# Selective scan of the last image: two-bank PSUM tiles of 1024 elements in place of four single banks

## The chip, the cores and the metric

The kernel runs on one core of one Trainium2 chip. The metric is the device time of one execution in microseconds (us); the time before is 25678.4 us, the median of three runs (25666.2 to 25685.54).

## The reference

The input is four images of 128 x 128 positions and 128 channels in float32. Two layers follow each other, each with a group norm in front and a residual around it.

```
x = x + L0(gn(x))     # deformable 3x3 convolution, two groups of 64 channels, bilinear sampling
x = x + L1(gn(x))     # two selective-scan (Mamba) blocks
```

The second layer takes each row of an image as one sequence: x has the shape (4, 128, 128, 128), and the reference reshapes it to 512 sequences of 128 steps. One scan block computes, for 256 inner channels and 16 states s,

```
delta = softplus(dt @ dtw + dtb);  dA = exp(delta * A[s])
h[t]  = dA[t] * h[t-1] + (delta*u)[t] * B[t, s]        # the scan
y[t]  = sum over s of h[t] * C[t, s];   out = ((y + u*D) * silu(res)) @ ow
```

## The kernel before

Layer 0 of image b + 1 is interleaved with layer 1 of image b. When the last image (b = 3) is in layer 1, no layer 0 is left, and layer 1 has the core to itself.

Layer 1 works in jobs. A job is one block of four rows (SR = 4, so TB = 512 positions) and one of the two scan layers. An image has 32 blocks, so the last image has 64 jobs. The jobs of two blocks alternate: block A layer 0, block B layer 0, A layer 1, B layer 1. Channels lie on the 128 partitions, in two halves c = 0, 1 (NC = 2).

- `pre` prepares a job: the input projection with the short convolution folded in (tile `pu`, L542, two groups of eight matmuls), silu (`u`), the gate `g` (`pr`, L557), the projections to dt, B and C (`pdb`, L566), their turned copy `bt`, then softplus in the steps L591 to L596 on ScalarE. Four dependent VectorE instructions end it: L600 (`e`), L601 and L602 (`de`, the delta), and L603 (`du`, delta times u).
- In the last image `turn_du` (L508) then turns `du` with TensorE (`pdu`) and ScalarE copies it to `duts` (L520).
- `main` does the scans of a job in eight quarters q of two states n (NQ = 2). A quarter has one of three `da` buffers. ScalarE fills it with exp (L639, four runs) and zeroes the first column of each row (L634), so that a scan starts afresh at each row.
- For n = 0 GpSimd multiplies `duts` by B into `xs` (L658, four instructions), for n = 1 ScalarE does (L656). TensorE turns `xs` into PSUM tile `px` (L663, four 128 x 128 transposes for each half c), and VectorE scans over 512 elements (L665).
- VectorE multiplies the quarter's 2048 results by C (L668), and TensorE adds them up in `y` (L133, sixteen transposes that accumulate).
- The tail of a job: gate (L689), turn back (`pyg`), output projection (`pout`), and for the second layer the residual and the store. The next job's `y` begins with `ddiag` times `u` (L618).

While `main` of a job runs, the `pre` of the next one is advanced by a step after each quarter, so that L600 to L603 stand near the sixth quarter and the pu groups near the first two. The tile framework decides the order on each engine's queue when the kernel is built, so the queues do not follow the program text strictly; each then runs in order and waits on semaphores. The next job's first `xs` need its `duts`, and so its L603.

PSUM has eight banks of 512 float32 per partition. In the kernel before, `ps` (two banks, tag "t") and `psa` (two banks, tag "acc") belong to layer 0; in the last image `px` takes them over, one bank per tile: `psa` for n = 0, `ps` for n = 1. `ps1` (two banks) serves `pre` and the tail, and `psy` (two banks) holds `y`. In the first three images a scan reads SBUF tile `hs` instead of PSUM and takes a quarter's 2048 elements at once (L679).

The layout of `da` is [c, n, s, t] in the kernel before, for every image.

Of the kernel before, what the change touches and what calls it, by code (L numbers as in the profile page):

```python
# [10 lines left out]
F32 = mybir.dt.float32  # L11
I32 = mybir.dt.int32
AF = mybir.ActivationFunctionType
ALU = mybir.AluOpType
PSUM = bass.MemoryType.PSUM
DRAM = bass.MemoryType.DRAM

P = 128
# [4 lines left out]
SR = 4  # L23
TB = SR * P
NGT = 4
NPA = 2
NL = 2
NC = 2
NS = 16
NQ = 2  # L30
# [34 lines left out]
def block_kernel(ctx: ExitStack, tc: tile.TileContext, a: dict, out: bass.AP):  # L65
    nc = tc.nc
# [9 lines left out]
    ident = const.tile([P, P], F32, name="ident")  # L76
# [13 lines left out]
    cw = ctx.enter_context(tc.tile_pool(name="w", bufs=1))  # L90
    small = ctx.enter_context(tc.tile_pool(name="small", bufs=1))
    pb = ctx.enter_context(tc.tile_pool(name="l0b", bufs=1))
    ps = ctx.enter_context(tc.tile_pool(name="l0ps", bufs=2, space=PSUM))
    psa = ctx.enter_context(tc.tile_pool(name="l0psa", bufs=NPA, space=PSUM))
    p2 = ctx.enter_context(tc.tile_pool(name="l1p2", bufs=1))
    pd = ctx.enter_context(tc.tile_pool(name="l1d", bufs=3, space=DRAM))
    ps1 = ctx.enter_context(tc.tile_pool(name="l1ps", bufs=4 - NPA, space=PSUM))
# [11 lines left out]
    offb, cbias, one, zero = misc[:, 0:1], misc[:, 1:2], misc[:, 2:3], misc[:, 4:]  # L109
# [21 lines left out]
    def add_transposed(o, v, start, stop):  # L131

        nc.tensor.matmul(o, v, ident, is_transpose=True, start=start, stop=stop, skip_group_check=True)  # L133
# [341 lines left out]
    NDA = 3  # L475
    n_da = [0]
    das, lm = [], []
# [13 lines left out]
    def next_h():  # L491
        n_h[0] += 1
        return hps[n_h[0] % NH]

    def load_x1(blk, nm):
        b, off = divmod(blk * TB, H * W)
        t = p2.tile([P, TB], F32, tag="x1t", name=f"x1t_{nm}", bufs=2)
        nc.sync.dma_start(t, x1[b][:, off : off + TB])
        return t

    def in_last(blk):

        return blk * SR // H == B - 1

    duts = []
    n_dut = [0]

    def turn_du(st, nm):  # L508

        if not duts:  # L510
            duts.append(lm[0].tile([P, 2, SR, NC * P], F32, tag="hs", name="duts"))
        n_dut[0] += 1
        dut = duts[0][:, n_dut[0] % 2]
        for k in range(SR // 2):
            pt = ps1.tile([P, 2, NC, P], F32, tag="t", name=f"pdu_{nm}_{k}")
            for i in range(2):
                for c in range(NC):
                    o = (2 * k + i) * P
                    nc.tensor.transpose(pt[:, i, c, :], st["du"][:, c, o : o + P], ident)
            nc.scalar.copy(dut[:, 2 * k : 2 * k + 2], pt.rearrange("p s c d -> p s (c d)"))  # L520
        st["dut"] = dut
# [88 lines left out]
    def main(st, l):  # L610

        blk = st["blk"]
        nm = f"{blk}_{l}"

        y = psy.tile([P, SR, NC, P], F32, tag="y", name=f"y_{nm}")
        for i in range(SR):
            for c in range(NC):
                nc.tensor.matmul(  # L618
                    y[:, i, c], st["u"][:, c, i * P : (i + 1) * P], ddiag[:, l, c, :],
                    start=(i % 2 == 0 and c == 0), stop=False, skip_group_check=True,  # L620
                )
        if in_last(blk) and "dut" not in st:
            turn_du(st, nm)
        for q in range(NS // NQ):
            bc = []
            for w in range(in_last(blk), 2):
                t = lm[0].tile([P, NQ, TB], F32, tag=f"bc{w}", name=f"bc{w}_{nm}_{q}", bufs=2)
                n0 = w * NS + q * NQ
                nc.sync.dma_start(t, st["bcd"][n0 : n0 + NQ, :].partition_broadcast(P))
                bc.append(t)  # L630
            da = das[n_da[0] % NDA]
            n_da[0] += 1

            nc.scalar.copy(da.rearrange("p c n s t -> p (c n s) t")[:, :, 0], zero)  # L634
            for c in range(NC):
                dv = st["delta"][:, c].rearrange("p (s t) -> p s t", s=SR)
                for n in range(NQ):
                    s = q * NQ + n
                    nc.scalar.activation(  # L639
                        da[:, c, n, :, 1:], dv[:, :, 1:], AF.Exp, scale=aneg[:, l, c, s : s + 1]  # L640
                    )
            dc = da.rearrange("p c n s t -> p c (n s t)")
            cv = bc[-1].rearrange("p n t -> p (n t)").unsqueeze(1).to_broadcast([P, NC, NQ * TB])
            if in_last(blk):


                for n in range(NQ):
                    s = q * NQ + n

                    xs = (lm[0] if n else pb).tile(  # L650
                        [P, SR, NC * P], F32, tag="bc0" if n else "gw", name=f"xs_{nm}_{s}", bufs=2
                    )
                    for i in range(SR):
                        bv = st["bt"][:, i, s : s + 1]
                        if n:
                            nc.scalar.activation(xs[:, i], st["dut"][:, i], AF.Copy, scale=bv)  # L656
                        else:
                            nc.gpsimd.tensor_scalar(xs[:, i], st["dut"][:, i], bv, None, ALU.mult)  # L658
                    for c in range(NC):
                        pool, tag = (ps, "t") if n else (psa, "acc")  # L660
                        px = pool.tile([P, SR, P], F32, tag=tag, name=f"px_{nm}_{s}_{c}")
                        for i in range(SR):
                            nc.tensor.transpose(px[:, i, :], xs[:, i, c * P : (c + 1) * P], ident)  # L663
                        dn = da[:, c, n].rearrange("p s t -> p (s t)")
                        nc.vector.tensor_tensor_scan(  # L665
                            dn, dn, px.rearrange("p s t -> p (s t)"), 0.0, ALU.mult, ALU.add
                        )
                nc.vector.tensor_tensor(dc, dc, cv, ALU.mult)  # L668
            else:
                hs = lm[0].tile([P, NC, NQ, TB], F32, tag="hs", name=f"hs_{nm}_{q}")  # L670

                for n in range(NQ):
                    nc.vector.scalar_tensor_tensor(  # L673
                        hs[:, :, n, :], st["du"], one,
                        bc[0][:, n].unsqueeze(1).to_broadcast([P, NC, TB]),
                        op0=ALU.mult, op1=ALU.mult,
                    )
                df = da.rearrange("p c n s t -> p (c n s t)")
                nc.vector.tensor_tensor_scan(  # L679
                    df, df, hs.rearrange("p c n t -> p (c n t)"), 0.0, ALU.mult, ALU.add  # L680
                )
                nc.vector.scalar_tensor_tensor(dc, dc, one, cv, op0=ALU.mult, op1=ALU.mult)  # L682
            for c in range(NC):
                for n in range(NQ):
                    for i in range(SR):
                        add_transposed(y[:, i, c], da[:, c, n, i, :], False, q == NS // NQ - 1 and n == NQ - 1)
            yield
        gt = st["g"]
        nc.vector.tensor_tensor(gt, y.rearrange("p s c d -> p s (c d)"), gt, ALU.mult)  # L689
        yg = p2.tile([P, NC, TB], F32, tag="yg", name=f"yg_{nm}")  # L690
        for c in range(NC):
            pt = ps1.tile([P, SR, P], F32, tag="t", name=f"pyg_{nm}_{c}")
            for i in range(SR):
                nc.tensor.transpose(pt[:, i, :], gt[:, i, c * P : (c + 1) * P], ident)  # L694
            nc.scalar.copy(yg[:, c], pt.rearrange("p s t -> p (s t)"))
        po = ps1.tile([P, TB], F32, tag="t", name=f"pout_{nm}")
        if l < NL - 1:
            for c in range(NC):
                nc.tensor.matmul(po, ow[:, l, c, :], yg[:, c], start=(c == 0), stop=(c == NC - 1))  # L699
            st["h"] = next_h()  # L700
            nc.scalar.copy(st["h"][:, :, DCONV - 1 :], po.rearrange("p (s t) -> p s t", s=SR))
        else:
            x1t = load_x1(blk, f"o{nm}")
            for i in range(SR):
                o = po[:, i * P : (i + 1) * P]
                nc.tensor.matmul(o, x1t[:, i * P : (i + 1) * P], ident, start=True, stop=False)
                for c in range(NC):
                    nc.tensor.matmul(  # L708
                        o, yg[:, c, i * P : (i + 1) * P], ow[:, l, c, :], start=False, stop=(c == NC - 1)
                    )  # L710
            ot = p2.tile([P, NC, TB], F32, tag="w1", name=f"ot_{nm}")[:, 0].rearrange("p (r c) -> p r c", r=SR)
            nc.scalar.copy(ot.rearrange("p r c -> p (r c)"), po)
            b, row = divmod(blk * SR, H)
            nc.sync.dma_start(out[b, row : row + SR].rearrange("r w c -> w r c"), ot)
# [121 lines left out]
```

## Time and profile before

| What | Value |
|---|---|
| Median of the runs | 25678.4 us (25666.2 to 25685.54) |
| Profiled execution | 25712.72 us, its span 25710.9 us |
| Mean granted TensorE clock | 0.891 of full speed |
| TensorE matmul busy | 20188.7 us, 79% of the span |
| VectorE busy | 20940.3 us, 81% |
| ScalarE busy | 16846.0 us, 66% |
| GpSimd busy | 18041.7 us, 70% |
| Scans of the last image (L665) | 2048 of 1202 ns on the mean, 21386 to 25693 us |

The engines are PE (TensorE matmul), PEld (its weight loads), DVE (VectorE), ACT (ScalarE), POOL (GpSimd) and SP (SyncE, which issues transfers). A line of the groups view gives the line of code, the engine, the operation, output and inputs, sizes and count; then the busy time in us and the mean duration of one in ns; and behind the second bar the idle time of the engine just before them, with what ended it. A line of the timeline gives the start, the length in us and, in brackets, the idle time before it and its releaser; neighbours of one kind are merged and counted with x. A duration is longer than the distance between two starts, since neighbours overlap a little.

### The profile page before, as it was taken

The numbers are of one execution on the slowest core, as the hardware profiler recorded it, in microseconds if no ns is written. First come the engines' busy times: TensorE is split into PE (matmuls) and PEld (weight loads), VectorE is DVE, ScalarE is ACT, GpSimd is POOL, SyncE is SP. The second block draws the span as 40 slices with busy tenths as digits, with TensorE's granted clock in tenths as the row PEclk, the third lists the DMA queues.
The fourth block names the chain that finished last, engine by engine and source line by source line (L and its number), as shares of the span: only waits on it lengthen the run. The fifth ranks groups of instructions, "written<-read, shape, count | busy, mean of one in ns | idle before, by whom it ended". The sixth has DMA issues, their size and how long they took to land. (4 is left out here: it accounts for less than half of the span.)

```text
span 25710.9 us, 302728 instructions
## 1 busy us (share of the span) xinstructions
PE 20188.7 (79%) x106276; PEld 12610.6 (49%) x106276; DVE 20940.3 (81%) x13054; ACT 16846.0 (66%) x40304; POOL 18041.7 (70%) x11270
## 2 busy tenths in 40 slices
PE   4676667888888887888888887888888877888787
PEld 2333334454554554554454454554554545666666
DVE  2212216999999999999999999999999998888888
ACT  2444445666676666666666666666676667888887
POOL 3666666788788885788788875888788864555555
PEclk7888888999998988999999988999999988999999
DMA  4434433444444544444444444444444442222222
GB/s 123 135 101 133 124 104 128 155 159 157 158 157 156 162 157 144 156 158 158 159 158 158 158 156 144 158 157 156 160 158 157 159 146 76 71 69 70 70 69 68
DMA packets 1530710, 3470.01 MB, mean 135 GB/s; under 512 B 243283, under 2 KB 717651, under 8 KB 1529052
## 3 DMA queue, kind: packets, MB, share of 16 engines
q1 hardware_dynamic: 1086812, 2242.08, 27.3%
q0 software_dynamic: 442368, 1208.55, 14.8%
q8 instruction: 835, 13.68, 0.2%
q14 instruction: 695, 5.69, 0.1%
HBM read 3299.19 MB, written 150.47 MB: 134 GB/s over the span
## 5 line engine op out<-in xcount | busy, mean ns | idle before, releaser
L365 POOL DMA_INDIRECT gt<-table,idx x9216 | 15685.9, 1702 | 5382.4 <-issue 2582.6
L679 DVE TENSOR_TENSOR_SCAN da<-da,hs 128x2048 f32<-128x2048 f32 x1536 | 6791.7, 4422 | 129.5 <-ACT da L639 32.3
L639 ACT ACTIVATE da<-de,aneg 128x508 f32<-128x508 f32 x8192 | 5478.4, 714 | 1879.2 <-PE y L133 1637.7
L422 PE MATMUL acc<-s,wc 128*64 128x512 f32 (+2 forms) x23520 | 6095.9, 616 | 685.3 <-ACT s L411 501.8
L133 PE MATMUL y<-ident,da 128*128 128x128 f32 x32768 | 4820.3, 308 | 2134.5 <-DVE da L682 1846.4
L133 PEld LDWEIGHTS y<-ident,da 128*128 128x128 f32 x32768 | 4303.0, 161 | 3108.4 <-DVE da L682 2070.9
L388 ACT ACTIVATE gw<-gt,wt 128x64 f32<-128x64 f32 x18432 | 4677.8, 342 | 760.5 <-DMA gt<-table,idx 290.7
L133 PE MATMUL p<-ident,gw 128*128 128x128 f32 x18432 | 2932.8, 306 | 1496.7 <-DVE gw L393 996.0
L658 POOL TENSOR_SCALAR xs<-duts,bt 128x256 f32<-128x256 f32 x2048 | 2355.1, 1166 | 2255.0 <-ACT duts L520 1191.9
L673 DVE SCALAR_TENSOR_TENSOR hs<-du,misc,bc 128x1024 f32<-128x1024 f32 x3072 | 3827.2, 1281 | 0.0
L422 PEld LDWEIGHTS acc<-s,wc 128*64 128x64 f32 (+1 forms) x23520 | 1787.3, 141 | 3972.9 <-issue 3315.2
L682 DVE SCALAR_TENSOR_TENSOR da<-da,misc,bc 128x2048 f32<-128x2048 f32 x1536 | 3608.8, 2349 | 32.5
L133 PEld LDWEIGHTS p<-ident,gw 128*128 128x128 f32 x18432 | 2385.8, 157 | 2417.2 <-DVE gw L393 965.1
L393 DVE TENSOR_TENSOR gw<-gt,wt 128x1024 f32<-128x1024 f32 x1152 | 1402.8, 1218 | 2304.6 <-DMA gt<-table,idx 821.0
L665 DVE TENSOR_TENSOR_SCAN da<-da,px 128x512 f32<-128x512 f32 x2048 | 2350.5, 1202 | 512.9 <-PE px L663 512.4
L411 ACT COPY s<-p 128x512 f32<-128x512 f32 x1152 | 671.6, 583 | 2246.0 <-PE p L133 1288.0
L542 PE MATMUL pu<-hp,inc 128*128 128x512 f32 x4096 | 1829.2, 593 | 0.2 <-ACT duts L520 0.2
L663 PE MATMUL px<-ident,xs 128*128 128x128 f32 x8192 | 1208.1, 287 | 529.0 <-DVE da L665 320.3
L663 PEld LDWEIGHTS px<-ident,xs 128*128 128x128 f32 x8192 | 967.6, 147 | 808.7 <-POOL xs L658 319.1
L668 DVE TENSOR_TENSOR da<-da,bc 128x2048 f32<-128x2048 f32 x512 | 1171.9, 2289 | 6.6
L542 PEld LDWEIGHTS pu<-hp,inc 128*128 128x128 f32 x4096 | 747.6, 190 | 810.8 <-issue 809.1
L408 ACT COPY s<-halo 128x256 f32<-128x256 f32 x1116 | 435.9, 404 | 995.3 <-PE acc L422 555.1
(138 smaller groups left out, 16188.5 us busy)
## 6 DMA issues: line engine op xcount, KB each, us to landing
bc<-bcd SPq DMA_DIRECT2D x3584, 512.0 KB
gt<-table,idx POOLq DMA_INDIRECT x9216
table<-xg SPq DMA_DIRECT2D x1016, 64.0 KB
xt<-in_x SPq DMA_DIRECT2D x124, 320.0 KB
xr<-in_x SPq DMA_DIRECT2D x128, 256.0 KB
x<-xo SPq DMA_DIRECT2D x128, 256.0 KB
x1t<-x SPq DMA_DIRECT2D x128, 256.0 KB
x1t_o<-x SPq DMA_DIRECT2D x128, 256.0 KB
```

The source lines that it names most:

```text
L133: nc.tensor.matmul(o, v, ident, is_transpose=True, start=start, stop=stop, skip_group_check=True)
L365: nc.gpsimd.indirect_dma_start(out=gt[:, v, r], out_offset=None, in_=flat, in_offset=bass.IndirectOffsetOnAxis(ap=idx[:, ri, o : o + 1], a ...
L388: nc.scalar.activation(gw[:, r, s, v], gts[h][:, v, r, s * CG : (s + 1) * CG], AF.Copy, scale=wt[:, u, r0 + r, s, v : v + 1],)
L422: nc.tensor.matmul(accs[b, j][CG * g : CG * g + CG, q, :], wc[sl, v, e, :], st[p + 4 * g if p < 4 else 8][sl, ky + q.start : ky + q.stop, ...
L542: nc.tensor.matmul(px.rearrange("p (s t) -> p s t", s=SR), inc[:, l, j, c * P : (c + 1) * P], h[:, :, j : j + P], start=(j == 0), stop=(j ...
L639: nc.scalar.activation(da[:, c, n, :, 1:], dv[:, :, 1:], AF.Exp, scale=aneg[:, l, c, s : s + 1])
L658: nc.gpsimd.tensor_scalar(xs[:, i], st["dut"][:, i], bv, None, ALU.mult)
L663: nc.tensor.transpose(px[:, i, :], xs[:, i, c * P : (c + 1) * P], ident)
L665: nc.vector.tensor_tensor_scan(dn, dn, px.rearrange("p s t -> p (s t)"), 0.0, ALU.mult, ALU.add)
L673: nc.vector.scalar_tensor_tensor(hs[:, :, n, :], st["du"], one, bc[0][:, n].unsqueeze(1).to_broadcast([P, NC, TB]), op0=ALU.mult, op1=ALU. ...
L679: nc.vector.tensor_tensor_scan(df, df, hs.rearrange("p c n t -> p (c n t)"), 0.0, ALU.mult, ALU.add)
L682: nc.vector.scalar_tensor_tensor(dc, dc, one, cv, op0=ALU.mult, op1=ALU.mult)
```

## The change

In the last image the `px` tile becomes [P, NC, SR, P], two neighbouring banks, and holds both halves c of one state. Two such tiles (pool `l1px`, bufs = 2) take the place of the four single banks; `ps` and `psa` are released before the first of them, and lie on the right side of PSUM so that the new pool can use their place. One scan of 1024 elements replaces two of 512. For this the last image views `da` as [n, c, s, t], so that both halves of a state are neighbours, and L668 takes C with a broadcast over c inside n. The number of transposes, exps, xs products and y additions stays as it was.

```diff
-    ps = ctx.enter_context(tc.tile_pool(name="l0ps", bufs=2, space=PSUM))
-    psa = ctx.enter_context(tc.tile_pool(name="l0psa", bufs=NPA, space=PSUM))
+    ps = tc.alloc_tile_pool(name="l0ps", bufs=2, space=PSUM, side="right")
+    psa = tc.alloc_tile_pool(name="l0psa", bufs=NPA, space=PSUM, side="right")
...
+        if in_last(blk) and not pxs:
+            psa.release()
+            ps.release()
+            pxs.append(
+                ctx.enter_context(
+                    tc.tile_pool(name="l1px", bufs=2, space=PSUM, side="right", reuse_waits="tile")
+                )
+            )
...
-            nc.scalar.copy(da.rearrange("p c n s t -> p (c n s) t")[:, :, 0], zero)
+            if in_last(blk):
+                da = da.rearrange("p c n s t -> p (c n s t)").rearrange(
+                    "p (n c s t) -> p c n s t", n=NQ, c=NC, s=SR
+                )
+
+            nc.scalar.copy(das[(n_da[0] - 1) % NDA].rearrange("p c n s t -> p (c n s) t")[:, :, 0], zero)
...
-            dc = da.rearrange("p c n s t -> p c (n s t)")
-            cv = bc[-1].rearrange("p n t -> p (n t)").unsqueeze(1).to_broadcast([P, NC, NQ * TB])
+            if in_last(blk):
+                dc = da.rearrange("p c n s t -> p n c (s t)")
+                cv = bc[-1].unsqueeze(2).to_broadcast([P, NQ, NC, TB])
+            else:
+                dc = da.rearrange("p c n s t -> p c (n s t)")
+                cv = bc[-1].rearrange("p n t -> p (n t)").unsqueeze(1).to_broadcast([P, NC, NQ * TB])
...
+                    px = pxs[0].tile([P, NC, SR, P], F32, tag="px", name=f"px_{nm}_{s}")
                     for c in range(NC):
-                        pool, tag = (ps, "t") if n else (psa, "acc")
-                        px = pool.tile([P, SR, P], F32, tag=tag, name=f"px_{nm}_{s}_{c}")
                         for i in range(SR):
-                            nc.tensor.transpose(px[:, i, :], xs[:, i, c * P : (c + 1) * P], ident)
-                        dn = da[:, c, n].rearrange("p s t -> p (s t)")
-                        nc.vector.tensor_tensor_scan(
-                            dn, dn, px.rearrange("p s t -> p (s t)"), 0.0, ALU.mult, ALU.add
-                        )
+                            nc.tensor.transpose(px[:, c, i, :], xs[:, i, c * P : (c + 1) * P], ident)
+                    dn = das[(n_da[0] - 1) % NDA].rearrange("p c n s t -> p (c n s t)")
+                    dn = dn[:, n * NC * TB : (n + 1) * NC * TB]
+                    nc.vector.tensor_tensor_scan(
+                        dn, dn, px.rearrange("p c s t -> p (c s t)"), 0.0, ALU.mult, ALU.add
+                    )
```

More of the change, by code (lines that the diff above doesn't have):

```diff
@@ L503, in in_last @@
         return blk * SR // H == B - 1
-    duts = []
+    duts, pxs = [], []
     n_dut = [0]
```

## Prediction

> **What bounds the kernel now.** First the 40 slices of the page: in the last seven POOL falls to 5 tenths, DMA to 2, and DVE stands at 8, not 9. This is the last image, in which layer 0 has ended and the edited branch runs (first L663 at 21382 us). The groups of lines in that window:
>
> ```profile
> L658 POOL TENSOR_SCALAR xs<-duts,bt 128x256 f32<-128x256 f32 x2048 | 2355.1, 1166 | 2255.0 <-ACT duts L520 1191.9 <-PE px L663 1063.1
> L665 DVE TENSOR_TENSOR_SCAN da<-da,px 128x512 f32<-128x512 f32 x2048 | 2350.5, 1202 | 512.9 <-PE px L663 512.4 <-ACT da L639 0.4
> L668 DVE TENSOR_TENSOR da<-da,bc 128x2048 f32<-128x2048 f32 x512 | 1171.9, 2289 | 6.6
> ```
>
> Read the part behind the second bar. DVE has the most work, yet stood idle 512 us, nearly all for px. Exps are never late (0.4 us). The timeline of DVE over one job (start, us, idle in brackets) says where:
>
> ```profile
> 24244.04 3.44 DVE L665 TENSOR_TENSOR_SCAN da<-da,px 128x512 f32<-128x512 f32 x3 [7.22 <-PE px L663]
> ...
> 24263.34 5.66 DVE L665 TENSOR_TENSOR_SCAN da<-da,px 128x512 f32<-128x512 f32 x5
> 24268.91 2.27 DVE L668 TENSOR_TENSOR da<-da,bc 128x2048 f32<-128x2048 f32 x1
> 24271.10 1.22 DVE L600 TENSOR_TENSOR e<-w,e 128x1024 f32<-128x1024 f32 x1
> 24272.23 1.21 DVE L665 TENSOR_TENSOR_SCAN da<-da,px 128x512 f32<-128x512 f32 x1
> 24273.36 1.20 DVE L601 TENSOR_TENSOR de<-de,e 128x1024 f32<-128x1024 f32 x1
> 24274.48 1.21 DVE L665 TENSOR_TENSOR_SCAN da<-da,px 128x512 f32<-128x512 f32 x1
> 24275.61 1.20 DVE L602 TENSOR_TENSOR de<-de,du 128x1024 f32<-128x1024 f32 x1
> 24276.72 1.22 DVE L665 TENSOR_TENSOR_SCAN da<-da,px 128x512 f32<-128x512 f32 x1
> 24277.85 1.20 DVE L603 TENSOR_TENSOR du<-de,u 128x1024 f32<-128x1024 f32 x1
> 24278.97 2.28 DVE L668 TENSOR_TENSOR da<-da,bc 128x2048 f32<-128x2048 f32 x1
> ...
> 24311.71 3.44 DVE L665 TENSOR_TENSOR_SCAN da<-da,px 128x512 f32<-128x512 f32 x3 [7.62 <-PE px L663]
> ```
>
> One long wait per job, in quarter 2; from there to L603 DVE is dense. The timelines of POOL and PE tell what follows L603:
>
> ```profile
> 24281.01 18.13 POOL L658 TENSOR_SCALAR xs<-duts,bt 128x256 f32<-128x256 f32 x16 [14.09 <-ACT duts L520]
> 24290.39 0.33 PE L663 MATMUL px<-ident,xs 128*128 128x128 f32 x1 [2.43 <-POOL xs L658]
> 24290.56 1.91 PE L133 MATMUL y<-ident,da 128*128 128x128 f32 x16
> ...
> 24311.00 1.47 PE L663 MATMUL px<-ident,xs 128*128 128x128 f32 x12
> ```
>
> So a job is a loop: DVE from the end of its wait to the end of du (24244.04 to 24279.05, 35.0 us); du turned and copied until POOL starts (2.0); eight xs of POOL for quarters 0 and 1 of the next job (9.4, until PE at 24290.39); PE with hardly a gap through y, px, the tail and both pu groups, until the next scan (21.3). The sum is 67.7 us, and starts of consecutive L689 lie 66.7 to 68.5 apart. DVE time behind L603 is not on the loop: its slack is the 7 us. **Only what stands between the wait and du, or in the PE chain, counts.** The dense 35.0 us are 19 scans at 1.115 start to start (21.2), four L668 at 2.21 (8.8), L600 to L603 at 1.13 (4.5), and 0.5 of small gaps.
>
> **The merged scan.** No 1024-element scan is in the trace. The 2048-element one of the earlier images (SBUF only) starts 4.33 us before what follows it:
>
> ```profile
> 12007.21 1.23 DVE L602 TENSOR_TENSOR de<-de,du 128x1024 f32<-128x1024 f32 x1
> 12008.35 4.42 DVE L679 TENSOR_TENSOR_SCAN da<-da,hs 128x2048 f32<-128x2048 f32 x1
> 12012.68 1.21 DVE L603 TENSOR_TENSOR du<-de,u 128x1024 f32<-128x1024 f32 x1
> ```
>
> Slope (4.33 - 1.115)/1536 = 2.093 ns an element; a scan of 1024 is 1.115 + 512 x 2.093 ns = 2.19 us against 2.23 for two: 43 ns saved. All 1024 merges would bring 44 us, 0.17%, less than the 0.2% (51 us) that a measurement of this kernel can tell from no change; on the loop 9.5 merges bring 0.4 us a job. Reading over two banks costs nothing: L689 reads 128x1024 from y, two banks, in 1204 ns, and L603, all SBUF, takes 1201.
>
> The Trainium skill (Perfetto Trace Analysis, Optimizing Scalar/DVE Operations) puts the overhead of a DVE instruction at about 125 ns with PSUM, and says that grouping helps if the engine is saturated. By its figure the loop would save 1.2 us, not 0.4. The same section advises breaking instructions up where DVE is not saturated and causes bubbles elsewhere; the 7 us wait per job is that case, and no run here has tried it.
>
> **What stands before du.** The order of each queue is fixed when the kernel is built, and the new one can't be read from this trace; I go by its habits. L600 to L603 depend on one another, and the queue puts one independent instruction between each two: in 63 of 64 jobs it reads L600, scan, L601, scan, L602, scan, L603. Length does not deter it: in the earlier image, above, the 4.42 us scan stands between L602 and L603. The fillers now double. Two merged scans of quarter 6 fill two places; their L668 fills the third, as it is ready by then. I also take both scans of quarter 2 behind the wait: today one of its four runs before it, which needs four transposes ahead of the tail, where now eight and a whole free pair are needed. That gives 10 x 2.19 + 5 x 2.21 + 4.5 = 37.4 against 34.5: **+2.9 us**. Bounds: nine scans and four L668 (no third filler, half of quarter 2 ahead), 33.0, -1.5; eleven scans (quarter 7 begun before L603), 39.6, +5.1. I take 2.9, since it keeps the pattern of the 63 jobs.
>
> **The two new waits.** A merged scan waits for its eighth transpose, not its fourth; on DVE the next scan, L668 and L689 queue behind it, and y, by way of L668, waits for them on PE. The first transpose of the next px waits for a whole pair, up to 1.1 us longer than for a bank; behind it on PE queue y and the pu, pdb and pdt groups of the next job, and ACT's u and e chain waits for those.
>
> **What PE does after du.** L668 of quarter 6 now ends before du, so its 16 y transposes (16 x 0.109 = 1.75 us) can stand before du's turn: 0 to +1.75, taken +0.6, for they have about 1.1 us of L603 to run in. Behind du, DVE has less left to quarter 7's L668, so y of quarter 7 may fall into PE's 2.43 us wait for POOL instead of behind it (24290.56, 1.91 us): -1.9 to 0, taken -1.0, half, as nothing decides. Eight transposes, not four, before the restarted scan: +4 x 0.109 = 0.44, paid back by four that leave the stretch before the tail: 0, at most +0.9.
>
> **Taken at nothing.** Exps: same runs of 127; the scan waits for the third exp instead of the first, 2 x 0.61 us later, but quarter 0's exps end at 24279.4, 6.7 us before its scan (24286.14). With that cover gone it costs 1.2 us. L668 on the new view: L393 with 64-element runs takes 1218 ns for 1024 elements against 1201, so at most 34 ns, 0.17 us a loop; runs of 512 are near the plain one. xs buffers come free at most 1.1 us later; in the dense part POOL works 4.66 of 6.8 us and waits 2.2. The hand-over of banks happens once, under the 12.09 us wait of the first scan for px: 0 to 12 us in all. SP's issues do not move.
>
> **Sum.** 2.9 + 0.6 - 1.0 = +2.5 us a job, times 63 = 158 us. The profiled execution took 25712.7 us (span 25710.9), so it would take 25871; it lies 34.3 above the median of 25678.4, so the forecast for the median is **25836 us**.
>
> By the skill's 125 ns the sum would be +1.7 a job, 25785.
>
> **Rivals.** *Slower still (0.20)*: dense quarters turn into lockstep. A pair is free only after the whole scan, so px of the next quarter may be queued behind y: then DVE waits 16 + 8 transposes, 24 x 0.109 = 2.6 us, each time. Against: a quarter gives DVE 6.8 us, and 32 transposes take PE 3.5. For: with pdb or pdt (1.9 us) only 1.4 is left, and PE already waits 320 us for scans to free banks. Once a job: 5.1 x 63 = 321, 26000 us. *Faster (0.20)*: du keeps its place (quarter 2 half ahead, L668 the third filler: 9 x 2.19 + 5 x 2.21 + 4.5 = 35.3, +0.75) and y of quarter 7 goes ahead of POOL's second group (-1.9): -1.15 x 63 = -72, **25606 us**. It decides at whether that L668 precedes the first scan of the next job: today that scan is first (24286.14, L668 at 24287.28). *No change (0.10)*: du moves neither way and only the 0.4 us remain: 25653 us. That the scan stays split, or a pair behaves as one buffer, I give 0.02, inside these.
>
> **Numbers.** The forecast has 0.50. The range is 25620 to 26000: it takes in the no-change case and half of each outer rival; the likeliest case's own is 25740 to 25950 (+1 to +4.3 a job). Faster 0.20, same 0.10, slower 0.70.
>
> **What would show it.** 1024 L665 of about 2.27 us; busy L665 near 2307 us (2350.5 less 44); between L600 and L603 two scans and an L668; L600 to the end of L603 near 11.1 us, not 8.0; L689 some 70 us apart. Wrong if L689 stays under 67.7 apart, or if 2.6 us waits for px stand in quarters 3 to 5.

## The result, and the profile after

| What | Before | After |
|---|---|---|
| Median of the runs | 25681.97 us (25637.43 to 25705.16, six runs) | 26149.85 us (26141.49 to 26177.95, six runs) |
| Span of the profiled execution | 25710.9 us | 26141.3 us |
| VectorE busy | 20940.3 us | 20947.0 us |
| Scans of the last image: busy, idle ahead | 2350.5 us, 512.9 us | 2302.9 us, 952.4 us |
| Start of L603 to the next start of L603, mean over the last image | 67.8 us | 75.0 us |

The ratio after to before is 1.0186, 95% interval 1.0173 to 1.0199: the changed kernel is slower by 1.9%, some 470 us. The 63 periods of 64 jobs grew by 7.2 us each, about 450 us, so the whole loss lies in the last image.

The groups of lines that answer to the three shown before (L674 is the old L658, L681 the old L665, L684 the old L668, L678 the old L663, L705 the old L689):

```profile
L674 POOL TENSOR_SCALAR xs<-duts,bt 128x256 f32<-128x256 f32 x2048 | 2381.4, 1182 | 2679.0 <-ACT duts L520 1435.4
L681 DVE TENSOR_TENSOR_SCAN da<-da,px 128x1024 f32<-128x1024 f32 x1024 | 2302.9, 2275 | 952.4 <-PE px L678 952.4
L684 DVE TENSOR_TENSOR da<-da,bc 128x2048 f32<-128x2048 f32 x512 | 1186.0, 2316 | 13.2
```

Ahead of the second bar all is as forecast: 1024 scans of 2275 ns, 47.6 us less work than 2048 scans of 1202 ns. Behind it the wait for `px` rose by 439.5 us. VectorE has no more to do than before; it waits more. The timeline of VectorE around one turn of the loop (start, length, idle time ahead and its releaser) says where:

```profile
24327.34 1.20 DVE L600 TENSOR_TENSOR e<-w,e 128x1024 f32<-128x1024 f32 x1
24328.57 1.23 DVE L601 TENSOR_TENSOR de<-de,e 128x1024 f32<-128x1024 f32 x1
24329.71 2.28 DVE L681 TENSOR_TENSOR_SCAN da<-da,px 128x1024 f32<-128x1024 f32 x1
24331.91 1.20 DVE L602 TENSOR_TENSOR de<-de,du 128x1024 f32<-128x1024 f32 x1
24333.03 2.28 DVE L684 TENSOR_TENSOR da<-da,bc 128x2048 f32<-128x2048 f32 x1
24335.23 1.22 DVE L603 TENSOR_TENSOR du<-de,u 128x1024 f32<-128x1024 f32 x1
24336.36 4.46 DVE L681 TENSOR_TENSOR_SCAN da<-da,px 128x1024 f32<-128x1024 f32 x2
...
24347.22 4.46 DVE L681 TENSOR_TENSOR_SCAN da<-da,px 128x1024 f32<-128x1024 f32 x2 [4.08 <-PE px L678]
24351.60 1.20 DVE L705 TENSOR_TENSOR g<-y,g 128x1024 f32<-128x1024 f32 x1
...
24364.03 2.29 DVE L681 TENSOR_TENSOR_SCAN da<-da,px 128x1024 f32<-128x1024 f32 x1 [6.83 <-PE px L678]
...
24371.43 4.46 DVE L681 TENSOR_TENSOR_SCAN da<-da,px 128x1024 f32<-128x1024 f32 x2 [2.78 <-PE px L678]
...
24388.12 2.29 DVE L681 TENSOR_TENSOR_SCAN da<-da,px 128x1024 f32<-128x1024 f32 x1 [0.89 <-PE px L678]
...
24404.70 2.29 DVE L681 TENSOR_TENSOR_SCAN da<-da,px 128x1024 f32<-128x1024 f32 x1 [0.69 <-PE px L678]
...
24411.36 4.46 DVE L681 TENSOR_TENSOR_SCAN da<-da,px 128x1024 f32<-128x1024 f32 x2
```

Where the kernel before had one long wait a job, there are now three: 4.08 us ahead of quarter 0 of the next job (0.43 before), 6.83 us ahead of the second scan of quarter 1, and 2.78 us ahead of quarter 2. Two shorter ones follow, 0.89 us in quarter 4 and, in about half of the jobs, 0.69 in quarter 6. L600 to the end of L603 takes 9.1 us here, 9.9 on the median of the jobs, against 8.0 before. The kernel before has these two lines where quarter 0 and the gate stand:

```profile
24286.14 1.22 DVE L665 TENSOR_TENSOR_SCAN da<-da,px 128x512 f32<-128x512 f32 x1 [0.43 <-PE px L663]
...
24293.93 1.20 DVE L689 TENSOR_TENSOR g<-y,g 128x1024 f32<-128x1024 f32 x1
```

The same turn on TensorE, behind L603, around the two pu groups and ahead of the wait in quarter 4:

```profile
24335.37 2.36 PE L133 MATMUL y<-ident,da 128*128 128x128 f32 x16 [2.16 <-DVE da L684]
24337.53 1.91 PE L519 MATMUL pdu<-ident,du 128*128 128x128 f32 x8
...
24344.89 0.48 PE L678 MATMUL px<-ident,xs 128*128 128x128 f32 x1 [3.21 <-POOL xs L674]
...
24348.41 2.91 PE L133 MATMUL y<-ident,da 128*128 128x128 f32 x16
...
24360.22 3.60 PE L542 MATMUL pu<-hp,inc 128*128 128x512 f32 x8
24363.66 0.27 PE L678 MATMUL px<-ident,xs 128*128 128x128 f32 x1
24363.76 3.60 PE L542 MATMUL pu<-hp,inc 128*128 128x512 f32 x8
...
24368.70 1.97 PE L133 MATMUL y<-ident,da 128*128 128x128 f32 x16 [1.12 <-DVE da L684]
24370.51 1.69 PE L678 MATMUL px<-ident,xs 128*128 128x128 f32 x14
...
24385.09 1.97 PE L133 MATMUL y<-ident,da 128*128 128x128 f32 x16 [1.79 <-DVE da L684]
...
24387.36 0.66 PE L678 MATMUL px<-ident,xs 128*128 128x128 f32 x4
```

The kernel before around its two pu groups:

```profile
24302.38 3.60 PE L542 MATMUL pu<-hp,inc 128*128 128x512 f32 x8
24305.82 1.91 PE L133 MATMUL y<-ident,da 128*128 128x128 f32 x16
24307.56 3.60 PE L542 MATMUL pu<-hp,inc 128*128 128x512 f32 x8
```

Two things are to be seen. `y` of quarter 6 now stands ahead of the turn of `du`, so `du` (ready at 24336.4) is turned from 24337.5 to 24339.4; before, the turn began 0.06 us after `du` and `y` stood behind it. And one single transpose of `px` (24363.66) stands behind the first pu group. The second scan of quarter 1 waits for it, L684 for that scan, `y` for L684, and the transposes of quarter 2 stand behind `y` on the queue. Before, that `y` stood between the two pu groups (24305.82) and quarter 2 restarted 0.55 us after the end of the second one; here it is 4.07 us after it.

Cut at the same four marks, one job of each kernel, all by starts on VectorE (the second column of the table is 24244.04, 24278.97, 24293.93, 24311.71; the third 24336.36, 24351.60, 24371.43, 24411.36; the scans of quarter 2 begin a turn, in the kernel before without the one of its four that ran ahead of the wait, and "end of du" is the start of what follows it):

| Stretch | Before | After | Change |
|---|---|---|---|
| Start of quarter 2's scans to the end of du | 34.9 us | 39.9 us | +5.0 |
| End of du to the gate L689/L705 | 15.0 us | 15.2 us | +0.3 |
| Gate to the start of quarter 2's scans | 17.8 us | 19.8 us | +2.0 |
| Sum | 67.7 us | 75.0 us | +7.3 |

In the second stretch the wait grew by 3.7 us, and the work fell by nearly as much, because the gate now stands behind fewer scans: two merged ones of quarter 0, where five single ones and a multiply stood between that wait and the gate.

Over 62 whole turns of the last image the same cut gives a plain account. From quarter 2's restart to the gate VectorE's time outside its waits is 49.5 us in the kernel before and 49.6 in the changed one: what moved ahead of `du` is missing behind it. The turn grew by 7.3 us in waits: ahead of quarter 0 from 0.47 to 3.99 us on the mean (+3.5), in quarters 4 and 6 from 0.06 to 1.95 (+1.9), and from the gate to quarter 2's restart from 17.51 to 19.35 (+1.8).

### The profile page after: what moved, and what is told of

It is laid out like the page before. It is cut to its first block, busy times and chain, and to the rows that moved or that the text cites. A ratio compares the mean times of both kernels' runs of the same rounds, so it can differ in the third digit from the quotient of the medians.

```text
span 26141.3 us, 301297 instructions
## 1 busy us (share of the span) xinstructions
PE 20367.8 (78%) x106276; PEld 12778.9 (49%) x106276; DVE 20947.0 (80%) x12030; ACT 16798.1 (64%) x40304; POOL 17954.4 (69%) x11270
## 5 line engine op out<-in xcount | busy, mean ns | idle before, releaser
L695 DVE TENSOR_TENSOR_SCAN da<-da,hs 128x2048 f32<-128x2048 f32 x1536 | 6790.2, 4421 | 129.1 <-ACT da L651 21.0
L651 ACT ACTIVATE da<-de,aneg 128x508 f32<-128x508 f32 x8192 | 5470.3, 711 | 2194.2 <-PE y L133 1760.0
L133 PE MATMUL y<-ident,da 128*128 128x128 f32 x32768 | 4878.4, 310 | 2351.0 <-DVE da L698 1816.0
L674 POOL TENSOR_SCALAR xs<-duts,bt 128x256 f32<-128x256 f32 x2048 | 2381.4, 1182 | 2679.0 <-ACT duts L520 1435.4
L689 DVE SCALAR_TENSOR_TENSOR hs<-du,misc,bc 128x1024 f32<-128x1024 f32 x3072 | 3826.6, 1280 | 0.0
L681 DVE TENSOR_TENSOR_SCAN da<-da,px 128x1024 f32<-128x1024 f32 x1024 | 2302.9, 2275 | 952.4 <-PE px L678 952.4
L678 PE MATMUL px<-ident,xs 128*128 128x128 f32 x8192 | 1307.4, 307 | 606.7 <-POOL xs L674 318.8
L678 PEld LDWEIGHTS px<-ident,xs 128*128 128x128 f32 x8192 | 1063.7, 158 | 920.8 <-POOL xs L674 440.4
L684 DVE TENSOR_TENSOR da<-da,bc 128x2048 f32<-128x2048 f32 x512 | 1186.0, 2316 | 13.2
```

Of the source, the lines that this page charges most:

```text
L651: nc.scalar.activation(da[:, c, n, :, 1:], dv[:, :, 1:], AF.Exp, scale=aneg[:, l, c, s : s + 1])
L678: nc.tensor.transpose(px[:, c, i, :], xs[:, i, c * P : (c + 1) * P], ident)
L681: nc.vector.tensor_tensor_scan(dn, dn, px.rearrange("p c s t -> p (c s t)"), 0.0, ALU.mult, ALU.add)
L689: nc.vector.scalar_tensor_tensor(hs[:, :, n, :], st["du"], one, bc[0][:, n].unsqueeze(1).to_broadcast([P, NC, TB]), op0=ALU.mult, op1=ALU. ...
L695: nc.vector.tensor_tensor_scan(df, df, hs.rearrange("p c n t -> p (c n t)"), 0.0, ALU.mult, ALU.add)
```

## The experiments

Times below stand beside the kernel before on the same chip (25746.38 us for the first four, 24932.08 for the next four, 25760.07 for the last two). Line numbers of their profiles are shifted by a few lines. A period is the mean over the last image from one start of `du` to the next, as in the first table (67.8 us before, 75.0 after).

**1. The view of `da` alone.** Single banks and scans of 512 as before, but the last image's new view of `da` and of C:

```diff
+            if in_last(blk):
+                da = da.rearrange("p c n s t -> p (c n s t)").rearrange(
+                    "p (n c s t) -> p c n s t", n=NQ, c=NC, s=SR
+                )
...
+                dc = da.rearrange("p c n s t -> p n c (s t)")
+                cv = bc[-1].unsqueeze(2).to_broadcast([P, NQ, NC, TB])
```

> Only the new view of da ([n, c, s, t]) and of C in L668 (here L676); the four single banks and the 512-element scans stay. Both theories on the scans (late last transposes, and pairs that come free as one) say the time of the kernel before: 25680 us, within 0.2%; L668's successor at 2.29 to 2.32 us, at most 17 us in all. If the view itself cost the time, 26150 us.

Measured: 25739.64 us, ratio 0.9998 (0.9989 to 1.0008), period 67.8 us, idle ahead of the scans 509.6 us. The view costs nothing that can be measured.

**2. Two-bank tiles, scans not merged.** The changed kernel, with two scans of 512 on each tile:

```diff
-                    dn = das[(n_da[0] - 1) % NDA].rearrange("p c n s t -> p (c n s t)")
-                    dn = dn[:, n * NC * TB : (n + 1) * NC * TB]
-                    nc.vector.tensor_tensor_scan(
-                        dn, dn, px.rearrange("p c s t -> p (c s t)"), 0.0, ALU.mult, ALU.add
-                    )
+                    for c in range(NC):
+                        dn = da[:, c, n].rearrange("p s t -> p (s t)")
+                        nc.vector.tensor_tensor_scan(
+                            dn, dn, px[:, c].rearrange("p s t -> p (s t)"), 0.0, ALU.mult, ALU.add
+                        )
```

> The two-bank tiles stay, so a pair still comes free only after its last scan, but each tile is read by two scans of 512 elements, and the first can start after four transposes. Theory A (the merged scan waits for its last transposes, which the queue order sets behind long groups of other matmuls): the loss goes, 25620 to 25780 us, waits of the scans for px near 510 us. Theory B (the pair comes free as one, so px cannot be made ahead): the loss stays, 26050 to 26150 us, waits near 950 us.

Measured: 25776.22 us, ratio 1.0009 (1.0000 to 1.0019), period 68.3 us, idle ahead of the scans 513.1 us. The hand-over of the banks, and their coming free in pairs, cost at most 0.2%. The loss comes with the merging of the scans.

**3 and 4. One state merged, the other not.** `half0` merges n = 0 (GpSimd's products) and keeps single banks for n = 1; `half1` the other way round. The merged state has one pair of banks (bufs = 1). The edit, with 0 for 1 in the second:

```diff
-                    px = pxs[0].tile([P, NC, SR, P], F32, tag="px", name=f"px_{nm}_{s}")
+                    if n == 0:
+                        px = pxs[0].tile([P, NC, SR, P], F32, tag="px", name=f"px_{nm}_{s}")
...
+                    else:
+                        for c in range(NC):
+                            pool, tag = (ps, "t")
+                            px = pool.tile([P, SR, P], F32, tag=tag, name=f"px_{nm}_{s}_{c}")
...
```

> Only the states whose xs GpSimd makes (n = 0) take a two-bank tile and a scan of 1024; n = 1 keeps two single banks and scans of 512. Theory A: the last transposes that PE left behind the pu group belonged to n = 1, so nothing is left behind here, 25620 to 25780 us. Theory B or a cost of each merged scan by itself: half of the loss, near 25915 us.

> Only the states whose xs ScalarE makes (n = 1) take a two-bank tile and a scan of 1024; n = 0 keeps two single banks. Its DVE queue has a scan of 512, a scan of 1024 and the multiply by C between L600 and L603 (5.5 us instead of 3.4), which the loop of the prediction prices at +2 us a job less what y gains in the wait for GpSimd (1.9). Theory A: 25650 to 25850 us. Theory B: half of the loss, near 25915 us; all of the loss (26150 us) if the scans of n = 1 alone set it.

Measured: `half0` 25777.85 us, 1.0010 (1.0001 to 1.0020), period 68.2 us; `half1` 26049.16 us, 1.0115 (1.0098 to 1.0132), period 72.7 us. The two do not add up to the 1.86% of both together, and `half1` lies outside each of the times that were expected of it. In `half0` the scans stood idle for `px` for 499 us over the last image (468.7 and 29.9 in its two groups), no more than before. The scan groups of `half1`:

```profile
L692 DVE TENSOR_TENSOR_SCAN da<-da,px 128x512 f32<-128x512 f32 x1024 | 1196.0, 1203 | 716.6 <-PE px L690 716.6
L682 DVE TENSOR_TENSOR_SCAN da<-da,px 128x1024 f32<-128x1024 f32 x512 | 1160.1, 2266 | 82.1 <-PE px L679 82.1
```

`half1` makes half of the merges and its merged scans hardly wait (82.1 us); the scans that wait are the 512-element ones of GpSimd's half. So late eighth transposes make at most 1.3 us a job of the 4.9 that the period grew. Its timelines on VectorE and TensorE say what makes most of the rest:

```profile
24294.24 2.28 DVE L682 TENSOR_TENSOR_SCAN da<-da,px 128x1024 f32<-128x1024 f32 x1
24296.44 1.20 DVE L603 TENSOR_TENSOR de<-de,du 128x1024 f32<-128x1024 f32 x1
24297.55 2.28 DVE L695 TENSOR_TENSOR da<-da,bc 128x2048 f32<-128x2048 f32 x1
24299.75 1.22 DVE L604 TENSOR_TENSOR du<-de,u 128x1024 f32<-128x1024 f32 x1
...
24311.95 2.33 DVE L692 TENSOR_TENSOR_SCAN da<-da,px 128x512 f32<-128x512 f32 x2 [4.12 <-PE px L690]
```

```profile
24299.89 3.68 PE L134 MATMUL y<-ident,da 128*128 128x128 f32 x16 [2.16 <-DVE da L695]
24303.36 1.63 PE L520 MATMUL pdu<-ident,du 128*128 128x128 f32 x8
```

The multiply of quarter 6 by C (L695) took the last gap ahead of `du` (L604), `y` of that multiply stands ahead of the turn of `du` (L520), and the next job's quarter 0 waits 4.12 us, as in the changed kernel; that wait stands in 62 of the 64 jobs. In `half0` quarter 6 still has three scans, which fill the three gaps, and the multiply stays behind `du`.

**5. Only the multiply of quarter 6 put behind `du`.** From here the theories were: C, `du` is turned late, because of what stands between L600 and L603; A, the scans' `px` is queued too late on TensorE; and that GpSimd's part sets the loop.

```diff
+                if q == 6 and not (blk == NB - 1 and l == NL - 1):
+                    with tc.issue_after(last_du[-1].ins):
+                        nc.vector.tensor_tensor(dc, dc, cv, ALU.mult)
```

> The changed kernel, with the multiply by C of quarter 6 queued behind L603 on VectorE, so that a scan of quarter 7 takes its place between L602 and L603. du comes no earlier, but the 16 y matmuls of quarter 6 no longer stand ahead of du's turn on PE (2.4 to 3.7 us there in the changed trace); the last px transpose of quarter 1 still stands behind the pu group. Theory C (the job is a loop through du, its turn and GpSimd, and du's turn is late): some 2 us a job less, ratio to the kernel before 1.011 to 1.015. Theory A (the transposes left behind the pu group set the time): as the changed kernel, 1.017 to 1.020.

Measured: 25410.15 us, 1.0189 (1.0172 to 1.0206), period 75.2 us: no gain. The queues of VectorE and of TensorE in its trace:

```profile
23522.24 2.28 DVE L682 TENSOR_TENSOR_SCAN da<-da,px 128x1024 f32<-128x1024 f32 x1
23524.44 1.20 DVE L604 TENSOR_TENSOR du<-de,u 128x1024 f32<-128x1024 f32 x1
...
23537.34 4.46 DVE L682 TENSOR_TENSOR_SCAN da<-da,px 128x1024 f32<-128x1024 f32 x2 [4.98 <-PE px L679]
```

```profile
23525.69 1.82 PE L520 MATMUL pdu<-ident,du 128*128 128x128 f32 x8 [3.27 <-DVE du L604]
...
23533.20 0.47 PE L679 MATMUL px<-ident,xs 128*128 128x128 f32 x1 [3.15 <-POOL xs L675]
23533.47 3.22 PE L133 MATMUL y<-ident,da 128*128 128x128 f32 x16
```

The place of the multiply was filled by a scan of quarter 7, also 2.2 us long, so `du` was no earlier, as expected. The turn of `du` now began right behind it (23525.69) in place of 1.1 us later, but `y` of quarter 6 then stood behind a transpose that waits 3.15 us for GpSimd, and the wait ahead of quarter 0 did not fall (4.98 us here). The 2 us a job that theory C expected of this edit did not come: `y` ahead of the turn of `du` is not by itself what costs the time. The long fillers ahead of `du`, the other half of theory C, were still there, and the run shows that a filler taken away is replaced.

**6. All transposes of `px` given priority on TensorE.** `with tc.high_priority():` around L678.

> The changed kernel, with its px transposes put ahead of all other matmuls that are ready when the queues are written. No transpose is left behind a pu group any more. Theory A: waits of the scans for px fall under 512 us and the time to 1.000 to 1.008 of the kernel before. Theory C: three instructions of 2.2 us still stand between L600 and L603, so 1.010 to 1.015. If late px had nothing to do with it: 1.019.

Measured: 25825.75 us, 1.0360 (1.0342 to 1.0377), period 82.0 us. Its scan group:

```profile
L682 DVE TENSOR_TENSOR_SCAN da<-da,px 128x1024 f32<-128x1024 f32 x1024 | 2304.3, 2277 | 1423.5 <-ACT da L651 723.3
```

The waits for `px` fell below 512 us as theory A said (413.6 us over the last image), but the time did not: now the scans wait 723.3 us for the exps of L651. In one turn the scans of quarters 3 to 5 wait 3.07, 5.72, 1.74 and 2.68 us for ScalarE. In the program an exp needs a free `da` buffer, and a buffer is free when `y` has read it; that `y` is late with `px` ahead of it agrees with ScalarE's wait for `y` ahead of the zeroing (L646), which rose from 362.0 to 481.4 us over the whole execution, but no run tries it alone. Fewer waits for `px` are not a shorter loop.

**7 and 8. GpSimd relieved.** ScalarE makes the products of quarter 1 for n = 0 too (`if n or q in (1,):`), in the kernel before and in the changed one.

> The kernel before, with the four xs of n = 0 in quarter 1 of the last image made by ScalarE (0.41 us each) instead of GpSimd (1.17 us). If the loop of the prediction holds (du, its turn, eight xs of GpSimd, the PE chain), its GpSimd part shrinks by up to 4.7 us a job and PE's wait of 2.4 us at that place goes: ratio 0.988 to 0.995. If GpSimd is not on the loop: 1.000 to 1.004 (ScalarE has 1.6 us a job more).

> The same move of quarter 1's xs to ScalarE in the changed kernel. Its trace shows PE waiting for GpSimd only for quarter 0, so the loop gains little there: 1.014 to 1.019 of the kernel before. If GpSimd's second group sets it, as in the kernel before: 1.006 to 1.012.

Measured: `before_act` 24880.57 us, 0.9981 (0.9972 to 0.9991), period 67.1 us; `after_act` 25342.84 us, 1.0165 (1.0148 to 1.0182), period 74.5 us. GpSimd's second four products (4.7 us) are half of its part of the loop that the prediction summed up. Taking them off it brought 0.7 us a job in the kernel before, between the two cases that were expected, and 0.6 in the changed one. In `before_act` the wait ahead of quarter 0 is gone (0.04 us on the mean of the turns, 0.47 before). So in the kernel before the loop through GpSimd is only just the longest; another chain, VectorE's dense work from quarter 2 to the gate (49.5 us) followed by the tail and the pu groups on TensorE (17.5 us), is shorter by that half microsecond. `before_act` is the one version here that is faster than the kernel before, by 0.19%.

**9 and 10. No long filler between the four steps.** The merged scan of quarter 6 for n = 1, the multiply of quarter 6 and the scans of quarter 7 for n = 0 are queued behind `du` of the next job:

```diff
+                    if (q, n) in ((6, 1), (7, 0)) and not (blk == NB - 1 and l == NL - 1):
+                        with tc.issue_after(last_du[-1].ins):
+                            nc.vector.tensor_tensor_scan(
+                                dn, dn, px.rearrange("p c s t -> p (c s t)"), 0.0, ALU.mult, ALU.add
+                            )
...
+                if q == 6 and not (blk == NB - 1 and l == NL - 1):
+                    with tc.issue_after(last_du[-1].ins):
+                        nc.vector.tensor_tensor(dc, dc, cv, ALU.mult)
```

> The changed kernel with one more edit: the second scan of quarter 6, the multiply of quarter 6 by C and the scans of quarter 7 for n=0 are queued on VectorE behind du of the next job, so that e, de and du stand next to each other without a long filler. Nothing is left out. Theory C (du's turn comes late, because a scan of 1024 elements and a multiply by C lie between the small steps and y of quarter 6 stands ahead of du's transposition; the scans of the next job's quarter 0 then wait 4.1 to 5.0 us): from the start of L600 to the end of L603 takes 5 to 7 us in place of 9.1, the wait of the next quarter 0 for px falls below 1 us, the job's period from 75.0 to 68-70 us, and the kernel to 1.000 to 1.010 of the kernel before. Theory that the merged scans by themselves, their late px or the pair of banks that comes free as one cost the time: the period stays at 74 to 75 us and the ratio at 1.016 to 1.019.

> The kernel that merges the scans of ScalarE's half (n=1) alone, with the same edit: the merged scan of quarter 6, the multiply of quarter 6 by C and the first scans of quarter 7 are queued behind du of the next job. Nothing is left out. Theory C: the wait of the next quarter 0 for px, 4.1 us in 62 of 64 jobs without the edit, falls below 1 us, the period from 72.7 to about 68.5 us, the ratio from 1.0115 to 1.000 to 1.004. Theory that merging ScalarE's half costs the time by itself: period and ratio stay at 72 to 73 us and 1.010 to 1.013.

Measured: `du_early` 25971.51 us, 1.0082 (1.0066 to 1.0099), period 71.2 us; `half1_du_early` 25854.62 us, 1.0039 (1.0027 to 1.0052), period 69.3 us. The edit takes back 1.04 of 1.86 per cent in the one and 0.76 of 1.15 in the other, so more than half of the loss was the order around `du`. The ratios lie in the ranges that theory C expected; the periods stayed above them. VectorE in `du_early`:

```profile
24431.33 4.46 DVE L688 TENSOR_TENSOR_SCAN da<-da,px 128x1024 f32<-128x1024 f32 x2 [8.56 <-PE px L679]
...
24449.56 2.29 DVE L688 TENSOR_TENSOR_SCAN da<-da,px 128x1024 f32<-128x1024 f32 x1 [2.43 <-PE px L679]
...
24462.99 1.20 DVE L601 TENSOR_TENSOR e<-w,e 128x1024 f32<-128x1024 f32 x1
...
24466.74 1.22 DVE L604 TENSOR_TENSOR du<-de,u 128x1024 f32<-128x1024 f32 x1
...
24486.06 1.19 DVE L716 TENSOR_TENSOR g<-y,g 128x1024 f32<-128x1024 f32 x1
```

The four steps take 5.0 us in place of 9.1, nothing waits between `du` and the gate in this turn (0.16 us on the mean of 62 turns, where the changed kernel has 3.99), and quarter 2 restarts right behind the second pu group. The stretches of the table above are now 36.6, 18.2 and 16.5 us. Of the 3.5 us that this turn is still longer than one of the kernel before, 2.43 are a wait in quarter 4 (1.6 us on the mean). The rest agrees with a coarser order ahead of the gate: from quarter 2 to the gate VectorE does 15 merged scans, the work of 30 single ones, where the kernel before does 28, so 2.2 us more stand ahead of the gate, and the 1.3 us that the stretch behind the gate is shorter gives part of it back. The 62 turns agree: 52.3 us of VectorE's time outside its waits from quarter 2's restart to the gate in place of 49.5, 1.8 us of waits in it in place of 0.5, and 17.0 us from the gate to quarter 2's restart in place of 17.5. No run tries these parts alone, nor do the two runs tell the fillers from the order of `y` and `px` on TensorE, which the edit changed too. But in `half1` the stretch from the gate to the restart is no longer than before (17.3 us), and there the edit took the wait ahead of quarter 0 from 4.2 to 0.4 us: that wait does not come from the left-over transpose.

## Why the prediction was wrong

The direction (slower, 0.70) held, and for the reason given: `du` comes later. The size did not: +158 us were forecast, +468 came, and 26149.85 lies above the range, which ended at 26000.

- **The merged scan: right.** 2.19 us from start to start and 44 us less work were forecast; the busy time fell by 47.6 us, 46 ns for each of the 1024 merges. The mean durations differ by more, 129 ns (twice 1202 less 2275), but neighbours overlap. The Trainium skill's overhead of about 125 ns (Perfetto Trace Analysis, Optimizing Scalar/DVE Operations) is not what a merge saved here.
- **What stands before du: right in its parts.** Ten merged scans, five L684 and the four small steps stand between quarter 2's start and the end of `du`, just as forecast. The gaps hold one scan and one L684 in place of two scans and one L684; the other scan stands directly ahead of L600, so the 11.1 us became 9.1 (9.9 on the median) while the count is the same. The stretch was to grow by 2.9 us and grew by 5.0: 1.6 of the rest are the two short waits for `px`.
- **The two new waits: priced at nothing, and the step that failed.** The text named them, and gave them no term in the sum. They cost 3.7 of the 7.3 us. The wait for the eighth transpose came in quarters 4 and 6, 1.9 us a job on the mean; in quarter 4 the last four transposes (24387.36) stand behind `y` (24385.09), as the rival "slower still" said they might. The other form was one left-over transpose behind a pu group, which by way of scan, L684 and `y` holds up quarter 2's transposes: its 2.78 us is the 2.6 us that the rival worked out (sixteen transposes of `y` and eight of `px`), and it stands once a job, as that rival said. It made the stretch from the gate to quarter 2's restart 1.8 us longer. Where it stands (quarter 2, behind pu) was not foreseen; the rival looked in quarters 3 to 5.
- **What PE does after du: wrong sign.** The two terms, +0.6 for `y` of quarter 6 and -1.0 for `y` of quarter 7, came to -0.4 us. From the end of `du` to quarter 2's restart the time went from 32.7 to 35.0 us, +2.3. `y` of quarter 6 did go ahead of the turn of `du` (+1.1 us until the turn began). `y` of quarter 7 did move ahead of quarter 1's transposes (24348.41, 2.91 us), but not into the wait for GpSimd: that wait (3.21 us at 24344.89) now stands ahead of quarter 0's transposes, with `y` behind it.
- **The view, the bank hand-over: right at nothing** (0.9998 and 1.0009).
- **The premise of one loop was wrong in one half.** The sum took VectorE's work behind `du` as free, with 7 us of slack. But in the kernel before VectorE waits only 0.5 us a turn between quarter 2's restart and the gate, so its work behind `du`, up to the gate, is as good as on the loop: that wait of 7 us is the end of the chain through gate, tail and pu groups, not room for more work ahead of it. Work that moves ahead of `du` costs only what quarter 0 waits longer: +3.5 us, where the forecast for that path was +2.5 (2.9 + 0.6 - 1.0). `du_early` moves work the other way and gets part of it back as a later gate.

So the forecast's parts were +2.9 and -0.4, and +5.0 and +2.3 were found. The rival "slower still", with a chance of 0.20, came nearest: it is the likeliest case and one wait of 2.6 us a job, 5.1 together, where the period grew by 7.2. Shown by runs is that the merging of ScalarE's half alone brings 1.15 of the 1.86 per cent (`half1`), and that the order around `du` makes more than half of it (`du_early`, `half1_du_early`); what the left-over transpose and the waits in quarters 4 and 6 cost is read from the traces alone.

## What to carry to other kernels

A merge of neighbouring instructions must be judged by what it does to the queue, not by its own 46 ns: it changes which instruction fills the gaps between dependent small steps, and which transposes are left behind a long group on another engine. Here the view and the banks were free, and the order around one 1.2 us step and one 0.1 us transpose cost most of the 1.9%. When a new wait can be named, give it a term in the forecast's sum; before work is called free, sum up what stands between two waits of the busiest engine; and when a filler is taken away, ask what the queue will put in its place.

## What was not expected of the hardware

The scan over two banks runs at the rate of one in SBUF: 2275 ns on the mean for 1024 elements, against 4421 ns for the 2048 of the earlier images and 1202 ns for 512 elements in one bank: 2.10 ns for each further element from 512 to 1024 as from 1024 to 2048. The mean granted clock of the span fell from 0.891 to 0.884 though TensorE is busy for a smaller share of it (79% to 78%). The whole fall lies in the last image (0.93 to 0.89 from 21400 to 25600 us; 0.88 ahead of it in both); no run here tells why. The matmuls of the pu groups took as long there as before (592 and 593 ns on the mean), so it is not what made the turn longer. And the kernel before takes 24932 us on one chip of this study and 25746 and 25760 us in the other two sessions, 3% apart (the granted clock was 0.90 there and 0.89 in the others), more than the effect that was measured: only runs on the same chip can be compared.
